# Shuffled pieces in one DMA issue, z beside x2 in alternate rows, a first half image in two steps, and a count read early

## The chip, the cores and the metric

The kernel runs on one core of one Trainium2 chip. The metric is device time in microseconds (us) of one execution; 0.2% of it is 5.9 us. The engines are named as in the profile: PE (matmul), PEld (weight load of the same engine), DVE (vector), ACT (scalar), POOL (GpSimd) and SP (which here issues most DMAs).

## The reference, cut

An activation x of shape (4, 256, 64, 64), float32, passes four layers, each with a residual:

```python
x = x + attention(gn(x))            # layer 0: axial attention, batch norms
x = x + ternary_conv3x3(gn(x))      # layer 1: weights -1, 0, 1
x = x + binary_block(gn(x))         # layer 2, below
x = x + conv3x3(gn(x), W)           # layer 3: weights built from 64x64

def binary_block(x):
    x = channel_shuffle(x, 2)
    xa, xb = split(x, 2, axis=1)
    x2 = batchnorm(leaky_relu(gconv3x3(sign(x), w1, groups=2)))
    x3 = batchnorm(concatenate((x2 + xa, xb), axis=1))
    x3 = channel_shuffle(x3, 2)
    x4 = batchnorm(leaky_relu(gconv3x3(sign(x3), w2, groups=2)))
    x5a, x5b = split(x3, 2, axis=1)
    return concatenate((x4 + x5a, x5b), axis=1)
```

`gn` is a group norm with 32 groups. A channel shuffle interleaves the two halves of the channels: new channel 2i is old i, new channel 2i + 1 is old 128 + i. The batch norms take their statistics over all four images, so each is a point where the whole of the data has to be there.

## The kernel before

Channels lie on partitions (128 of them, P), so the 256 channels make two halves, t = 0 and 1; a channel half of one image is 128 x 4096 float32 (HW = 4096), held in two tiles of 128 x 2048. The four images are b = 0 to 3.

The attention of layer 0 leaves its two parts in DRAM, `at_d[0]` and `at_d[1]`. Layers 1 and 3 are one function, `conv_layer`, named "d" and "g", a Winograd convolution along the rows. For every image `prepare(b, t)` loads a channel half through `load_1` or `load_3`, sums its statistics (L1028 for the sum; L1086 and L1088 in the trace are the aggregate and the shift of its mean), `norm` turns these into a scale over groups with small matmuls into `pst` (L112, L122, L123), `transform` writes a padded half image (ACT, L1110) and its row transforms `dtr` or `gtr` (DVE, L963 to L976), and `chunk` runs the matmuls (L989, `dc` or `gc`), adds the results to the residual on DVE and calls `finish`. `rest()` runs the chunks of an image with the preparation of the next between them. For the first image all of `prepare`, `norm` and `transform` has to be done before the first matmul of the layer, in two steps: g begins with the channel half t = 1, d with t = 0, and the first 36 or more matmuls need that half only.

`load_1` (d) brings x in shuffled order with `load_shuffled` (L138 to L143), which issues two DMAs of 64 rows into alternate partitions; then, for `two` in 0 and 1, eight pieces of 128 x 512 of the attention's output, also through `load_shuffled`, each followed by one DVE operation (L1181). The pieces have tags a0 and a1 by their number, with two buffers each. `finish_1` stores the layer's result to `x2_d` (L1204) by POOL.

Layer 2 (names e_...) has two binary convolutions. A half image of signs lies in `e_pad`; `binary_rows` (L1241) makes its row transforms `e_tr` on DVE, four operations of 128 x 1056 for each of the two groups; `binary_conv` runs 72 matmuls a chunk (L1251) and six DVE operations (L1260 to L1266), one ACT copy and one ACT square. `images` runs four chunks an image with `prepare_1` or `prepare_2` of the next image between them. `rows_of` loads 33 rows of x2 into one of four slots (three of pool xp3, the fourth, every fourth load, of xp1). In `prepare_2` (L1450 to L1469) the half t = 1 gives signs only (L1468); t = 0 is scaled by ACT (L1455), gets the first convolution's result added by DVE (L1459), is stored to `z_d` (L1462, 128 rows), and gives signs. Both halves' signs go to both groups, and only then come the row transforms. All this needs the batch norm's affine after the last chunk of the first convolution (end of it L1408).

`load_3` (g) brings a half of x2 (L1494), then four times a piece of z and x2 in alternate partitions:

```python
a = ap_.tile([P, HW // 8], F32, name=f"x3_{b}_{t}_{half}_{q}", tag="a0")
nc.sync.dma_start(out=a[0:P:2, :], in_=z_d[b][64 * t : 64 * t + 64, part])
nc.sync.dma_start(out=a[1:P:2, :], in_=x2_d[b][P + 64 * t : P + 64 * t + 64, part])
nc.vector.scalar_tensor_tensor(
    xt[:, cols], a, sg[:, t, 0, b : b + 1], xt[:, cols], ALU.mult, ALU.add
)
```

(L1500 to L1505), all with tag a0, that is two buffers; for t = 0 a piece of y follows with tag a1 (L1507 to L1516).

The order on each engine is set by a scheduler that places instructions by priority and readiness as it models them; `tc.high_priority()`, `tc.keep_in_program_order(i)` and `tc.issue_after(i)` constrain it. A DMA waits on its issuing queue for its buffer, and whatever is behind it on that queue waits with it.

At the end a count of attention rows whose softmax sum left the safe range is formed (one matmul, one cast), read into registers on the engines, and compared: only if it is above zero is everything from the scores on done again in a general form. It is zero here, so that second copy isn't run.

Of the kernel before, what the change touches and what calls it, by code (L numbers as in the profile page):

```python
# [18 lines left out]
B = 4  # L19
# [21 lines left out]
def network(ctx: ExitStack, tc, x, wqkv, relm, relt, relw, relv, counts, masks, vecs, rowv, ab, w1, l2w1, l2w2, l3w, mats, out):  # L41
# [16 lines left out]

    at_d = [[scratch(f"at_d{two}{b}", [C, HW]) for b in range(B)] for two in range(2)]
    x2_d = [scratch(f"x2_d{b}", [C, HW]) for b in range(B)]  # L60
    z_d = [scratch(f"z_d{b}", [P, HW]) for b in range(B)]
    y_d = [scratch(f"y_d{b}", [P, HW]) for b in range(B)]

    u1_d = scratch("u1_d", [P, 2, 3, 6, C])
# [71 lines left out]
        nc.vector.tensor_tensor(c, beta, c, ALU.subtract)  # L136
        return s, c

    def load_shuffled(dst, src, t, step=P):

        for par in range(2):
            r = par * step + 64 * t
            nc.sync.dma_start(out=dst[par:P:2, :], in_=src[r : r + 64, :])  # L143

    def kernel_rows(u, w, a, c):

# [520 lines left out]
    def from_scores(general, keep):  # L667
# [487 lines left out]
        with ExitStack() as ph:  # L1155
            shift = {}

            def load_1(b, t, xh, ap_, st, mv, sp, pst, spare):
                for half in range(2):
                    load_shuffled(xh[half], x[b][:, bass.ts(half, HW // 2)], t)  # L1160
                for two in range(2):
                    if b == 0:
                        if t == 1:
                            prs[t, two] = value_norm(t, two, pst, "pst")
                    for half in range(2):
                        for q in range(4):
                            k = 4 * half + q
                            a = ap_.tile([P, HW // 8], F32, name=f"a_{b}_{t}_{half}_{q}_{two}", tag=f"a{q % 2}")
                            if two == 0:
                                load_shuffled(a, at_d[0][b][bass.ts(t, P), bass.ts(k, HW // 8)], 0, 64)  # L1170
                                xv = xh[half][:, bass.ts(q, HW // 8)]
                                av = a
                            else:

                                load_shuffled(
                                    a, at_d[1][b][bass.ts(t, P), q * 1024 + half * 512 : q * 1024 + half * 512 + 512], 0, 64
                                )
                                xv = xh[half].rearrange("p (n i) -> p n i", i=64)[:, :, bass.ts(q, 16)]
                                av = a.rearrange("p (n i) -> p n i", i=16)
                            kw = {"accum_out": st[:, k, 0:1]} if b == 0 and two == 1 else {}  # L1180
                            nc.vector.scalar_tensor_tensor(  # L1181
                                xv, av, prs[t, two][:, 0:1], xv, ALU.mult, ALU.add, **kw
                            )
                            if kw:
                                cols = slice(16 * q, 16 * q + 16)
                                nc.scalar.activation(
                                    spare[:, 1:33, 1 + 16 * q : 17 + 16 * q], xh[half].rearrange("p (n i) -> p n i", i=64)[:, :, cols],
                                    AF.Square, accum_out=st[:, k, 1:2],
                                )
                        if two == 1 and b > 0:  # L1190
                            half_stats(st, half, xh[half])
                if b == 0:
                    whole_stats(sp, mv, st)
                    shift[t] = small(keep, [P, 1])
                    nc.vector.tensor_tensor(shift[t], prs[t, 0][:, 1:2], prs[t, 1][:, 1:2], ALU.add)
                return shift[t], b == 0

            st_x2 = {}

            def finish_1(b, h, co, xh, sp, pst):  # L1200
                if h == 0:
                    st_x2[b, co] = sp.tile([P, NB, 6], F32, name=f"stx2_{b}_{co}", tag=f"sx{co}")
                half_stats(st_x2[b, co], h, xh)
                nc.gpsimd.dma_start(out=x2_d[b][bass.ts(co, P), bass.ts(h, HW // 2)], in_=xh)  # L1204
                if h == 1:
                    nc.vector.bn_aggr(mv2[:, b, co, :], st_x2[b, co].rearrange("p k s -> p (k s)"))
                    if co == 1:
                        gm, rs = norm_stats(sp, pst, mv2[:, b], slice(0, 2), M_GRPS, "2")
                        nc.vector.tensor_copy(gm2[:, b, :], gm)
                        nc.vector.tensor_copy(rs2[:, b, :], rs)  # L1210

            set_up, load_weights, prepare, norm, transform, rest, sp, pst = conv_layer(
                "d", ph, u1_d, "x0 a p0 x1 t0 u0 x2 x3 s u1 o x4 t2 t3 t1 x5 t4 t5 p1", M_GRPS, load_1,
                vec[:, V_L1B : V_L1B + 2], (0, 1), finish_1,
            )
            set_up()
            prepare(0, 0)
            load_weights(0, nc.sync)
            with tc.high_priority():
                norm(0, slice(0, 1))  # L1220
            transform(0, 0, 0)
            prepare(0, 1)
            load_weights(1, nc.sync)
            norm(0, slice(1, 2))
            transform(0, 1, 0)
            for t in range(2):
                transform(0, t, 1, True)
            rest()

        def binary_rows(v, pad):

            d = [pad[:, r : r + 31 : 2, :] for r in range(4)]
            for k, (i, j, op) in enumerate(
                ((0, 2, ALU.subtract), (1, 2, ALU.add), (2, 1, ALU.subtract), (1, 3, ALU.subtract))
            ):  # L1240
                nc.vector.tensor_tensor(v[:, k], d[i], d[j], op)  # L1241

        def binary_conv(psp, lp, parts, vs, q, dst, sums, squares, name):

# [26 lines left out]
        with ExitStack() as ph:  # L1271
# [51 lines left out]
            def inside(t, h, rows=slice(0, P)):  # L1323
                return pads[t][h][rows, 1 - h : 34 - h, 1:65]

            def transformed(b, t, h, i):
                s = 2 * ((2 * (B * i + b) + 1 - i + h) % 3) + t
                v = tslots[s].tile([P, 4, 16, 66], BF16, name=f"e_tr{i}_{b}_{t}_{h}", tag="tr")
                binary_rows(v, pads[t][h])
                return v  # L1330

# [116 lines left out]
            nc.vector.tensor_tensor(sa, sy1, half_scales(0, cy1), ALU.mult)  # L1448


            def prepare_2(b, h):
                for t in (1, 0):
                    xt = rows_of(b, t, h, "x3")
                    if t == 0:
                        nc.scalar.activation(  # L1455
                            xt, xt, AF.Identity, bias=cx[:, 0, b : b + 1], scale=sx[:, 0, b : b + 1]
                        )
                        xf = xt.rearrange("p h w -> p (h w)")
                        nc.vector.scalar_tensor_tensor(  # L1459
                            xf, y[b][:, 64 * 31 * h : 64 * (31 * h + 33)], sa, xf, ALU.mult, ALU.add  # L1460
                        )
                        nc.gpsimd.dma_start(out=z_d[b][:, bass.ts(h, HW // 2)], in_=xf[:, 64 * h : 64 * h + HW // 2])  # L1462
                    for g in range(2):
                        src = xt[64 * g : 64 * g + 64]
                        kw = {} if t == 0 else {
                            "bias": cx[64 * g : 64 * g + 64, 1, b : b + 1], "scale": sx[64 * g : 64 * g + 64, 1, b : b + 1]
                        }
                        nc.scalar.activation(inside(g, h, slice(64 * t, 64 * t + 64)), src, AF.Sign, **kw)  # L1468
                return [transformed(b, g, h, 1) for g in range(2)]  # L1469

            def chunk_2(b, q, vs):
                binary_conv(
# [14 lines left out]
        with ExitStack() as ph:  # L1487
            shift_y = small(keep, [P, B])

            def load_3(b, t, xh, ap_, st, mv, sp, pst, spare):  # L1490
                first = b == t == 0
                for half in range(2):
# [4 lines left out]
                    for q in range(4):  # L1497
                        part = bass.ts(4 * half + q, HW // 8)
                        cols = bass.ts(q, HW // 8)
                        a = ap_.tile([P, HW // 8], F32, name=f"x3_{b}_{t}_{half}_{q}", tag="a0")  # L1500
                        nc.sync.dma_start(out=a[0:P:2, :], in_=z_d[b][64 * t : 64 * t + 64, part])
                        nc.sync.dma_start(out=a[1:P:2, :], in_=x2_d[b][P + 64 * t : P + 64 * t + 64, part])
                        nc.vector.scalar_tensor_tensor(
                            xt[:, cols], a, sg[:, t, 0, b : b + 1], xt[:, cols], ALU.mult, ALU.add
                        )  # L1505
# [38 lines left out]
            for t in (1, 0):  # L1544
                transform(0, t, 1, True)
            rest()
        return bad

    bad = from_scores(False, keep)

    with ExitStack() as ph:
        sp = pool(ph, "z_s")
        far = small(sp, [P, 1])
        nc.vector.tensor_scalar(far, bad, -float(P), float(P), ALU.mult, ALU.add)
        count = sp.tile([1, 1], mybir.dt.int32, name="count")
        with ExitStack() as sums:
            psp = pool(sums, "z_ps", 1, PSUM)
            ps = psp.tile([P, 1], F32, name="pbad", tag="pbad")
            nc.tensor.matmul(ps[0:1], lhsT=far, rhs=mt[:, M_ALL, 0:1], start=True, stop=True)
            nc.vector.tensor_copy(count, ps[0:1])  # L1560
        lost = nc.values_load(count[0:1, 0:1], min_val=0, max_val=P)
        with tc.If(lost > 0):
            with ExitStack() as again:
                from_scores(True, pool(again, "z_keep"))


def _matrices():
# [107 lines left out]
```

## Time and profile before

| | us |
|---|---|
| median of 3 runs | 2942.96 (2942.49 to 2944.54) |
| profiled execution | 2940.49 |
| its span in the trace | 2938.6 |
| PE busy in the span | 2603.1 |
| DVE busy | 2050.6 |
| ACT busy | 1055.2 |
| granted PE clock, mean | 0.949 of full speed |

The span runs from the first to the last recorded instruction. "Busy" is the time with an instruction on the engine; for SP it isn't given, since issuing DMAs isn't counted as work. Stretches are quoted by their times in the span: attention ends near 1540, d runs to 2078, the first binary convolution to 2230, the second to 2392, g to the end.

### The profile page before, as it was taken

To read this page: it belongs to the slowest core of one execution; us is meant where nothing else is said; L and a number is where in the kernel's file an instruction comes from. 1 tells how busy PE (TensorE), PEld (TensorE's weight loads), DVE (VectorE), ACT (ScalarE), POOL (GpSimd) and SP (SyncE) were. 2 spreads that over 40 slices of the span, in tenths; PEclk is the share of its full clock that TensorE was granted. 3 is DMA by queue.
4 is the path that set the end of the run, shared out by engine and by line. 5 is a ranking of instruction groups with operands and counts; after the bars stand their busy time and mean duration, and the time that the engine had idled before them with its cause. 6 is when DMAs were issued, how large, how long until landed. Compare 5 with 4: busy or idle time off the path is not lost.

```text
span 2938.6 us, 77718 instructions
## 1 busy us (share of the span) xinstructions
PE 2603.1 (89%) x34248; PEld 1599.4 (54%) x34248; DVE 2050.6 (70%) x3661; ACT 1055.2 (36%) x2029; POOL 79.1 (3%) x153
## 2 busy tenths in 40 slices
PE   7999889899999688878766999999996968999997
PEld 4566556677777476666663444444453533444443
DVE  6555997566676356666667898895687968858742
ACT  4554445455555644454423011021247621110100
POOL 0000000000000100000000000000000000000000
PEclk9998999999999799989987999999997988999999
DMA  6767465555454877777774533432336763333100
GB/s 237 261 213 218 136 191 144 139 138 133 125 118 111 237 248 248 250 235 246 261 241 161 185 120 125 154 118 87 103 106 216 256 222 118 108 111 136 65 40 34
DMA packets 250266, 484.45 MB, mean 165 GB/s; under 512 B 29056, under 2 KB 129024, under 8 KB 225088
## 3 DMA queue, kind: packets, MB, share of 16 engines
q1 hardware_dynamic: 182304, 293.90, 31.3%
q10 hardware_dynamic: 58336, 125.85, 15.3%
q0 software_dynamic: 9280, 59.64, 5.1%
q8 instruction: 271, 4.44, 0.6%
q14 instruction: 75, 0.61, 0.1%
HBM read 282.96 MB, written 196.35 MB: 163 GB/s over the span
## 4 chain that ended last, share of the span: by engine, by line
PE 27%; issue 22%; DVE 7%; DMA 6%; ACT 3%; POOL 0%; SPq 0%; ACTq 0%; POOLq 0%; DVEq 0%
PE dc L989 15%; PE pc L1251 4%; DMA at_d<-o_False 3%; PE e_False L790 2%; PE den_False L841 2%; DVE pt L800 2%; PE pe_False L893 2%; DMA qc_False<-q_d 1%; PE pr_False L859 1%; PE pa_False L868 1%; ACT pt L830 1%; DVE o_False L877 1%; DMA x<-x_d 1%; ACT e_pad L1468 1%; ACT rb L861 1%
## 5 line engine op out<-in xcount | busy, mean ns | idle before, releaser
L989 PE MATMUL dc<-dtr,d_u 128*128 128x512 f32 x1152 | 504.6, 599 | 15.0 <-issue 9.6
L989 PE MATMUL gc<-gtr,g_u 128*128 128x512 f32 x1152 | 502.5, 598 | 11.7 <-DVE gtr L967 7.1
L479 DVE STREAM_TRANSPOSE t<-pd 128x1024 f32<-128x1024 f32 x256 | 303.9, 1226 | 107.7 <-PE pd L472 107.7
L989 PEld LDWEIGHTS gc<-gtr,g_u 128*128 128x128 f32 x1152 | 219.1, 191 | 287.7 <-issue 271.5
L989 PEld LDWEIGHTS dc<-dtr,d_u 128*128 128x128 f32 x1152 | 218.2, 191 | 285.8 <-issue 274.4
L472 PE MATMUL pd<-rm,qb 64*32 64x256 f32 x8192 | 283.5, 386 | 45.7 <-DVE t L479 42.6
L491 PEld LDWEIGHTS pq<-t,t 64*64 64x64 f32 x8192 | 258.8, 135 | 71.6 <-issue 48.5
L491 PE MATMUL pq<-t,t 64*64 64x64 f32 x8192 | 278.4, 220 | 17.5 <-issue 15.6
L1251 PE MATMUL pc<-e_tr,e_k 128*64 128x512 bf16 x2304 | 262.7, 388 | 19.3 <-DVE e_tr L1241 16.2
L495 ACT ACTIVATE o<-pq 128x512 f32<-128x512 f32 x256 | 152.2, 595 | 314.2 <-PE pq L491 314.1
L472 PEld LDWEIGHTS pd<-rm,qb 64*32 64x32 f32 x8192 | 156.6, 108 | 128.2 <-DVE t L479 60.8
L830 ACT ACTIVATE pt<-pt,sm 128x512 f32<-128x512 f32 x256 | 162.2, 709 | 174.1 <-DVE pt L800 174.1
L1251 PEld LDWEIGHTS <-e_k 128*64 128x64 bf16 x2304 | 144.8, 111 | 134.0 <-issue 24.7
L800 DVE TENSOR_TENSOR pt<-e_False,si_False 128x1024 f32<-128x1024 f32 x128 | 151.3, 1215 | 36.3 <-PE e_False L790 33.6
L790 PE MATMUL e_False<-qc_False,rw 32*128 32x256 f32 x1024 | 130.0, 469 | 31.5 <-DVE pt L800 19.2
L500 ACT ACTIVATE pq<-pq 128x512 f32<-128x512 f32 x256 | 149.8, 585 | 3.9
L1007 ACT COPY gc_c<-gc 128x512 f32<-128x512 f32 x32 | 18.6, 581 | 336.6 <-PE gc L989 336.4
L1007 ACT COPY dc_c<-dc 128x512 f32<-128x512 f32 x32 | 18.6, 583 | 327.0 <-PE dc L989 327.0
L280 PE MATMUL po<-xg,wt 128*128 128x512 f32 x256 | 123.2, 621 | 6.7 <-DVE st L287 5.1
L893 PE MATMUL pe_False<-pt,ve 128*32 128x64 f32 x4096 | 89.8, 239 | 41.9 <-issue 38.0
L295 PE MATMUL pv<-wt,xg 128*128 128x256 f32 x512 | 119.9, 382 | 0.0
L295 PEld LDWEIGHTS pv<-wt,xg 128*128 128x128 f32 x512 | 96.5, 191 | 33.4 <-issue 19.2
(399 smaller groups left out, 3385.2 us busy)
## 6 DMA issues: line engine op xcount, KB each, us to landing
si_False<-qk_d SPq DMA_DIRECT2D x64, 1024.0 KB
qk_d<-o ACTq DMA_DIRECT2D x124, 512.0 KB
x<-x_d SPq DMA_DIRECT2D x32, 1056.0 KB
a<-at_d SPq DMA_DIRECT2D x256, 128.0 KB
xa<-in_x SPq DMA_DIRECT2D x16, 1024.0 KB
vt_d<-vs ACTq DMA_DIRECT2D x32, 512.0 KB
q_d<-qs SPq DMA_DIRECT2D x64, 256.0 KB
qb<-q_d SPq DMA_DIRECT2D x128, 128.0 KB
```

Of the source, the lines that this page charges most:

```text
L295: nc.tensor.matmul(pv[:, j, :], lhsT=xg[:, t, pix], rhs=wt[:, t, C : 2 * C], start=(t == 0), stop=(t == 1),)
L472: nc.tensor.matmul(pds[t][32 * c : 32 * c + 32, m].rearrange("p j k -> p (j k)"), lhsT=q[rows, 2 * (gp % 2) + g, a, 32 * nb : 32 * nb + 32 ...
L479: nc.vector.transpose(ts[t][:, :, 32 * jh : 32 * jh + 32].rearrange("p a j b -> p j a b"), pds[t].rearrange("p m j k -> p j m k"),)
L491: nc.tensor.matmul(ps[rows, m, :], lhsT=ts[1][rows, n // 2, :, n % 2], rhs=ts[0][rows, n // 2, :, n % 2], start=True, stop=True, tile_posi ...
L495: nc.scalar.activation(o[:, :, 8 * k : 8 * k + 8, :], ps.rearrange("p n (a b) -> p a n b", b=2), AF.Copy, accum_out=acc[:, 0, gp, col : co ...
L500: nc.scalar.activation(psf, psf, AF.Square, accum_out=acc[:, 1, gp, col : col + 1])
L790: nc.tensor.matmul(es[x_ // 2][:, x_ % 2, :, :, par], lhsT=rw[rows, 63 - i : 127 - i].rearrange("p j r -> p (j r)"), rhs=q[rows, :, par, k ...
L800: nc.vector.tensor_tensor(dst, e, src, ALU.add)
L830: nc.scalar.activation(s, s, AF.Exp, scale=s2q[:, gp : gp + 1])
L893: nc.tensor.matmul(ps[32 * a : 32 * a + 32, m // 2, :, m % 2], lhsT=ve[:, 63 - i, :], rhs=pt[:, i // 2, a, :, i % 2], start=True, stop=Tru ...
L989: nc.tensor.matmul(ms[k], lhsT=u[t][:, dx, k, bass.ts(co, P)], rhs=vs[t][:, k, :, dx : dx + 64], start=(first and dx == 0), stop=(last and ...
L1251: nc.tensor.matmul(m[64 * g : 64 * g + 64], lhsT=parts[:, g, i, k, dx, :], rhs=vs[g][:, k, 8 * (q % 2) : 8 * (q % 2) + 8, dx : dx + 64], s ...
```

## The change

Four edits:

- `load_shuffled` is one DMA of 128 rows, whose source is a view that takes rows i and 64 + i (or 128 + i) in turn.
- `z_d` has 256 rows. z goes to its even rows, and `finish_1` stores the upper half of x2 a second time, to the odd rows (by POOL). So `load_3` takes a piece in one DMA of 128 rows. The tags of its t = 1 pieces alternate between a0 and a1, four buffers in all; t = 0 pieces stay in a0, beside y in a1.
- `prepare_2` loads t = 0 first, makes the signs of t = 1 first, and does the rest for the first half image of the first image in two steps of 16 or 17 rows: scale, add, signs and eight of the 16 row pairs each. `issue_after` holds the same work of each later half image behind the one before it. z is stored once a half image, after the steps.
- The count's matmul, cast and reading stand directly after d instead of at the end.

```diff
-    z_d = [scratch(f"z_d{b}", [P, HW]) for b in range(B)]
+    z_d = [scratch(f"z_d{b}", [C, HW]) for b in range(B)]
...
-    def load_shuffled(dst, src, t, step=P):
-        for par in range(2):
-            r = par * step + 64 * t
-            nc.sync.dma_start(out=dst[par:P:2, :], in_=src[r : r + 64, :])
+    def load_shuffled(dst, src, t):
+        rows = src.rearrange("(two i) f -> i two f", two=2)[64 * t : 64 * t + 64]
+        nc.sync.dma_start(out=dst, in_=rows)
...
                 nc.gpsimd.dma_start(out=x2_d[b][bass.ts(co, P), bass.ts(h, HW // 2)], in_=xh)
+                if co == 1:
+                    nc.gpsimd.dma_start(
+                        out=z_d[b].rearrange("(p two) f -> two p f", two=2)[1][:, bass.ts(h, HW // 2)], in_=xh
+                    )
...
             rest()
+            lost = None
+            if not general:
+                far = small(keep, [P, 1])
+                nc.vector.tensor_scalar(far, bad, -float(P), float(P), ALU.mult, ALU.add)
+                ps = pst.tile([P, 1], F32, name="pbad", tag="pst")
+                nc.tensor.matmul(ps[0:1], lhsT=far, rhs=mt[:, M_ALL, 0:1], start=True, stop=True)
+                count = keep.tile([1, 1], mybir.dt.int32, name="count")
+                nc.vector.tensor_copy(count, ps[0:1])
+                lost = nc.values_load(count[0:1, 0:1], min_val=0, max_val=P)
...
-        def binary_rows(v, pad):
-            d = [pad[:, r : r + 31 : 2, :] for r in range(4)]
+        def binary_rows(v, pad, first=0, n=16):
+            d = [pad[:, r + 2 * first : r + 2 * first + 2 * n - 1 : 2, :] for r in range(4)]
...
             def prepare_2(b, h):
-                for t in (1, 0):
-                    xt = rows_of(b, t, h, "x3")
-                    if t == 0:
+                xts = [rows_of(b, t, h, "x3") for t in range(2)]
...
+                signs(1, slice(0, 33))
+                vs = [slot(b, g, h, 1) for g in range(2)]
+                steps = ((0, 17, 0), (17, 33, 8)) if b == h == 0 else ((0, 33, 0),)
+                n = 16 // len(steps)
+                with ExitStack() as order:
+                    for i in ahead:
+                        order.enter_context(tc.issue_after(i))
+                    for r0, r1, pair in steps:
+                        xt = xts[0][:, r0:r1]
                         nc.scalar.activation(
                             xt, xt, AF.Identity, bias=cx[:, 0, b : b + 1], scale=sx[:, 0, b : b + 1]
                         )
                         xf = xt.rearrange("p h w -> p (h w)")
                         nc.vector.scalar_tensor_tensor(
-                            xf, y[b][:, 64 * 31 * h : 64 * (31 * h + 33)], sa, xf, ALU.mult, ALU.add
+                            xf, y[b][:, 64 * (31 * h + r0) : 64 * (31 * h + r1)], sa, xf, ALU.mult, ALU.add
                         )
+                        sign = signs(0, slice(r0, r1))
+                        for g in range(2):
+                            row = binary_rows(vs[g], pads[g][h], pair, n)
+                ahead[:] = [sign.ins, row.ins]
+                nc.gpsimd.dma_start(
+                    out=z_d[b].rearrange("(p two) f -> two p f", two=2)[0][:, bass.ts(h, HW // 2)],
+                    in_=xts[0].rearrange("p h w -> p (h w)")[:, 64 * h : 64 * h + HW // 2],
+                )
+                return vs
...
-                        a = ap_.tile([P, HW // 8], F32, name=f"x3_{b}_{t}_{half}_{q}", tag="a0")
-                        nc.sync.dma_start(out=a[0:P:2, :], in_=z_d[b][64 * t : 64 * t + 64, part])
-                        nc.sync.dma_start(out=a[1:P:2, :], in_=x2_d[b][P + 64 * t : P + 64 * t + 64, part])
+                        a = ap_.tile([P, HW // 8], F32, name=f"x3_{b}_{t}_{half}_{q}", tag=f"a{t * q % 2}")
+                        nc.sync.dma_start(out=a, in_=z_d[b][bass.ts(t, P), part])
```

`signs(t, rows)` makes both groups' signs of those rows, with the scale and shift of t = 1 in the same operation; `slot` is the tile allocation that `transformed` did.

## The prediction, made before the changed kernel was run

> **What bounds the kernel now.** I read the page first (which engine is full), then busy time by stretch (where it is not), then the waits of those stretches, then the DVE's timeline inside them.
>
> ```profile
> PE 2603.1 (89%) x34248; PEld 1599.4 (54%) x34248; DVE 2050.6 (70%) x3661; ACT 1055.2 (36%) x2029; POOL 79.1 (3%) x153
> a<-at_d SPq DMA_DIRECT2D x256, 128.0 KB
> x<-z_d SPq DMA_DIRECT2D x64, 128.0 KB
> x<-x_d SPq DMA_DIRECT2D x64, 128.0 KB
> ```
>
> The PE is 89% busy, so a saving counts only where the PE stands still. By stretch (PE first, DVE third, the PE's clock near the end):
>
> ```profile
> 1540.00:1600.00 60.00, 31.29 (x67) 15.17 (x68) 42.28 (x121) 20.90 (x43) 0.00 (x0) 0.69 0.62 202
> 1600.00:1700.00 100.00, 99.76 (x237) 44.06 (x236) 89.14 (x160) 12.17 (x15) 1.70 (x3) 1.00 0.47 147
> 2205.00:2250.00 45.00, 18.24 (x129) 10.94 (x127) 33.02 (x81) 27.38 (x24) 1.59 (x3) 0.67 0.50 174
> 2250.00:2360.00 110.00, 109.33 (x990) 63.87 (x986) 97.61 (x173) 79.51 (x66) 5.85 (x11) 1.00 0.76 268
> 2360.00:2440.00 80.00, 44.73 (x196) 20.96 (x197) 57.56 (x144) 19.76 (x36) 0.00 (x0) 0.74 0.60 207
> 2440.00:2920.00 480.00, 479.43 (x1129) 211.93 (x1128) 317.75 (x552) 50.72 (x61) 7.98 (x15) 1.00 0.25 85
> ```
>
> Both Winograd layers run full once begun. The PE misses 29, 27 and 35 us at three joints: start of the ternary layer (d), turn from the first to the second binary convolution, start of the last layer (g). The change touches all three. Waits of the last joint (2340 to 2440; total, times, longest):
>
> ```profile
> PE pst L112 <- DVE sm L1088: 22.8, 2, 12.7
> DVE gx L1503 <- DMA x<-x_d: 13.6, 6, 4.4
> PE gc L989 <- DVE gtr L967: 7.1, 1, 7.1
> DVE gx L1503 <- DMA gx<-x_d: 5.6, 2, 3.3
> DVE gx L1513 <- DMA yq<-y_d: 4.4, 3, 4.0
> SPq L1501 <- DVE gx L1503: 24.0, 10, 7.6
> ```
>
> The last row is the cause of the second: SP issues nothing until the DVE gives a piece buffer back. The DVE's timeline, with its idle times:
>
> ```profile
> 2357.40 0.75 DVE L1503 SCALAR_TENSOR_TENSOR gx<-x,sg,gx 128x512 f32<-128x512 f32 x1 [4.39 <-DMA x<-x_d]
> ...
> 2365.88 0.75 DVE L1503 SCALAR_TENSOR_TENSOR gx<-x,sg,gx 128x512 f32<-128x512 f32 x1 [2.74 <-DMA x<-x_d]
> 2368.65 0.75 DVE L1503 SCALAR_TENSOR_TENSOR gx<-x,sg,gx 128x512 f32<-128x512 f32 x1 [2.02 <-DMA x<-x_d]
> ...
> 2376.26 0.15 DVE L1088 TENSOR_TENSOR sm<-sm,sg 128x1 f32<-128x1 f32 x1
> ```
>
> Two pieces, a round trip, two pieces; then L1088, and 0.20 us later the PE.
>
> **What the Trainium skill says.** "DMA: Bandwidth & Descriptors", Anatomy of one DMA, gives about 2.0 us plus bytes over 436e9 per second for a transfer: as an estimate 2.3 us for 128 KB, 2.6 for 256 KB, so one issue of 128 rows should land about when two of 64 do. The trace agrees in a quiet moment (two 256 KB yq loads whose issues ended near 2413.0 and 2413.5 were used at 2415.11 and 2416.13, 2.1 and 2.6 us) but not in traffic: the pair of 64-row loads issued up to 2361.25 was used at 2368.65, 7.4 us. The same page, "Issuing engines are not separate DMA queues", says SP, ACT and POOL transfers share 16 engines; so the 8 MB more written by POOL load the SP's reads. "Perfetto Trace Analysis", DMA Instruction — HWDGE, says the profiled window of an issue leaves out the movement; hence landings here are read at the waiting instruction.
>
> **The change part by part.** I worked from the order of instructions that the changed program has on each engine.
>
> *Stage A, start of d.* L143 issues a piece twice, 0.54 us each; now once: 128 x 0.54 = 69 us of SP less over the layer, 16 dx issues too. SP isn't the bound except at the start. Before, the first sum (L1088, 1552.39) came after the last t=0 pieces at 1548.7 and 1550.1, which waited for loads, nine pieces standing after the attention's last statistics (1540.4). In the new order five pieces go ahead of the first L877, into DVE idle time (3.26 us before 1506.64 alone), and only two stand after the last statistics. What remains behind 1540.4: two pieces 1.5, L713 and small ones 1.9, square and sum about 1: L1088 near 1544.7, 7.7 earlier, and dc from 1559 instead of 1565.80.
> That stretch of 42 matmuls (21.1 us) then needs the other channel half. Its L1088 stood at 1584.74, behind seven pieces 1574.0 to 1582.4 paced by loads (idle 1.90, 0.55, 0.65, 0.39, 0.52, 1.73 between them). Without that pacing they end near 1570.5. But in the new order 12 pieces of image 1 and 3 or 4 statistics (12 x 0.68 + 3 x 0.65, about 10 us of DVE) stand between the sum and the row transform L963, where none stood. L963 thus comes near 1583 instead of 1591.39, the PE resumes near 1586 instead of 1593.51: **-7** (0 if image 1's pieces wait for loads; -10 if they don't queue up).
>
> *z in alternate rows.* prepare_2 stores z to even rows; finish_1 adds eight 1 MB POOL stores for the odd rows: 8 x 0.53 = 4.2 us of a POOL that is 97% idle. A dx buffer is freed one store later, 4.2 us from issue to landing (the x_d<-dx row); the PE has full work beside it there (DMA share 0.47 or less). Taken 0; were that cover gone, 4.2 per image, at most 13.
>
> *Stage B, end of the first binary convolution.* A late load landed at 2218.15, its two signs took 4.31 on ACT, and the copy for the last chunk ran behind them at 2223.68. In the new order that slot's load comes earlier and only one sign (2.15) stands there: 1.5 to 3, taken **-2**.
>
> *Stage C, second binary convolution.* The affine is done at 2234.4 (L1408). Before: 3 Identities (2.07 each), 3 L1459 (2.36 each) in a row, signs, rows; PE at 2244.45, then a 1.0 us wait. Half images halve each link: 1.12 + 1.27 + 2 signs 1.03 + rows 0.33, PE after about 5.4 instead of 10. But from 2236.6 to 2343.95 the DVE is about 95% busy with 7.4 us of preparing and 3.7 us a chunk, so the PE would soon wait for it: of 4.6 only about **-1** stays (0 to -5). Eight more small operations at 0.06 overhead add 0.5 to the DVE, inside this.
>
> *Stage D, start of g.* Tags a0/a1 alternate, so four buffers instead of two for t=1, and one issue a piece (0.45 + 0.60 before). All four pieces of the first half are there when the DVE arrives at 2343.95; the next four are in flight during those and a chunk (3.74), with one round trip of up to 7 us instead of three. Of the idle 4.39 + 2.74 + 2.02 = 9.2 most goes: L1088 near 2366.5, -9.5. The PE's wait of 10.04 for it goes with that; the next, gc at 2396.52, moves to 2387. Then the t=0 half: its yq round trips (last pair issued until 2418.10, used at 2422.60, behind a 1 MB gx load issued at 2414.84). In the new order that gx load precedes the pairs, and z needs half the issues: second L1088 2414 instead of 2426.12, gc resumes 2424.5 instead of 2436.60: -12 in all since the affine; of these the DVE's earlier end from C is 1. **-10** here without it (-5 to -14).
>
> *Count.* PE gets one 128x1 matmul at the d-to-e joint (L112 0.59 for two), 0.3 with its wait for the PSUM; SP waits for the cast about 2 us before the e_k of the second convolution, needed 150 us later; the TensorLoads on other engines stay at the end, so only matmul and cast leave there: **+0.2**.
>
> Sum: -7 - 2 - 1 - 10 + 0.2, about -20; I take -18, since C and D share the DVE. Span 2938.6 to about 2920.6, profiled run 2940.49 (1.9 around the span) to 2922.5; the median 2942.96 lies 2.5 over that run, so **2925**.
>
> **Rivals.**
> 1. *One joint pays only.* For: stage A's ten us of image-1 pieces are read from an order, and their loads may not have landed (before, 8 waits of 6.8 us for a<-at_d); stage D's yq buffers stay two. Against: SP has 69 us less to issue. A gives 0 and D -5 to -7 with B, C -2: -8, **2935**.
> 2. *The joints give all.* Image 1's pieces don't delay (-10), C's 4.6 stays: -27, **2916**.
> 3. *Slower: the one-issue shuffled load lands late.* Its rows come from two halves of the source, and if that costs, 20 pieces (8 of image 0, 12 of image 1) stand ahead of L963 at d's start with four buffers. At landing time T a piece comes every T/4 + 0.4. From about 1545, 20 pieces reach 1591 at 2.3 each, that is T = 7.6: from there A loses. With T = 12: 3.4 each, 68 us, PE resumes at 1615, +21, and D keeps -10 + 2 x 5 = 0: **2962**. Against: the longest landing read before is 7.4, in the heaviest stretch (share 0.76), and at d's start 0.62.
> 4. *The change doesn't do what it says:* the early count leaves the end as it was (the last TensorLoads follow the last store anyway); that is in the forecast.
>
> **How the numbers follow.** Forecast -18: 0.60. Joints give all: 0.08. One joint only: 0.19. Slower: 0.13. A measurement here tells 0.2% (5.9 us) from nothing: faster below 2937.1, slower above 2948.9. Rival 1 falls two thirds under the bound. Faster 0.60 + 0.08 + 0.12 = 0.80, same 0.08, slower 0.12. Range 2911 to 2940: rival 2 and rival 1 with their spread inside, rival 3 left out.
>
> **What would show it.** A: d's first pst L112 near 1545, dc's second stretch from about 1586, a<-at_d x128. B: no 4.3 us pair of signs at the end of pc1. C: first pc2 within 6 us of L1408. D: four L1544 (the old L1503) in a row, L1088 near 2366 less A, B and C, its wait on the PE under 3. Wrong if the PE's wait before pst at g is still near 10, if DVE idles for a<-at_d over 10 us at d's start, or if dc or gc have gaps inside their full stretches.

## The result, and the profile after

The changed kernel took 2939.97 us (median of 20 runs, 2926.74 to 2962.07), the one before 2942.72 in as many runs beside it: ratio 0.9989, 95% interval 0.9972 to 1.0007. That is no change that the measurement can tell from none, where 18 us less were forecast. The profiled execution took 2933.51, its span is 2931.7, 6.9 less than the span before; the interval says that this difference is not one to build on.

The page of the changed kernel: engines (busy time, share, instructions), and two lines of its DMA issues.

```profile
PE 2600.8 (89%) x34248; PEld 1595.5 (54%) x34248; DVE 2046.4 (70%) x3670; ACT 1056.1 (36%) x2032; POOL 83.2 (3%) x161
a<-at_d SPq DMA_DIRECT2D x128, 256.0 KB
```

The issues are halved as written, and the PE is as full as it was. Busy time by stretch, in the columns of the prediction (PE first, DVE third):

```profile
1540.00:1600.00 60.00, 37.74 (x86) 17.35 (x87) 51.75 (x132) 15.76 (x30) 0.00 (x0) 0.79 0.67 224
1600.00:1700.00 100.00, 97.59 (x228) 43.25 (x227) 83.68 (x152) 14.01 (x16) 2.22 (x4) 0.98 0.33 116
2205.00:2250.00 45.00, 29.71 (x240) 18.12 (x238) 34.23 (x91) 29.59 (x24) 1.06 (x2) 0.81 0.52 186
2250.00:2360.00 110.00, 100.11 (x902) 56.35 (x896) 99.61 (x179) 75.90 (x66) 6.38 (x12) 1.00 0.75 272
2360.00:2440.00 80.00, 45.08 (x155) 20.57 (x156) 56.24 (x138) 17.86 (x34) 0.00 (x0) 0.70 0.54 188
2440.00:2920.00 480.00, 474.61 (x1120) 209.98 (x1118) 311.98 (x543) 50.12 (x60) 8.51 (x16) 1.00 0.23 85
```

The gain and the loss can both be read here. At d's start the PE works 6 us more in the 60, at the turn of the two binary convolutions 11 more in the 45. But the two stretches that were full are full no longer: 97.6 of 100 in d, and 100.1 of 110 in the second binary convolution, where it was 109.3. (The last row is lower for another reason: the changed kernel's last matmul ends at 2914.6, inside the stretch.)

The waits of the last joint (2340 to 2440; total, times, longest):

```profile
PE pst L113 <- DVE sm L1088: 25.1, 2, 17.9
DVE gx L1544 <- DMA x<-z_d: 6.2, 4, 2.4
PE gc L989 <- DVE gtr L967: 6.7, 1, 6.7
DVE gx L1544 <- DMA gx<-x_d: 6.0, 1, 6.0
DVE gx L1554 <- DMA yq<-y_d: 6.0, 4, 3.1
```

The wait of the DVE for its pieces has halved (13.6 to 6.2). The PE's wait for L1088 hasn't shrunk in sum (22.8 to 25.1): the first of the two went from 10.0 to 7.1, the second from 12.7 to 17.9.

Single executions of one kernel spread over some 30 us. The traces say where much of this lies: the last den matmuls of the attention stand between 1489.1 and 1507.1 in the sixteen traces of this study, although the DVE's order up to there is the same in all. (SP's isn't quite: where `load_shuffled` issues once, three issues of x stand before that point instead of six.) What follows it repeats better where the program is the same (d's start 93.1 to 94.3 in the eight traces of kernels that leave it alone). So the traces are compared stage by stage from the last den matmuls (1499.3 before, 1493.6 after), each stage between two events on the PE or the DVE. `den` are the attention's softmax sums, `pc` the sums of a binary convolution, `psg` the small matmuls with scale and shift between the two; d's full stretch begins when the second channel half is there.

| us | before | changed |
|---|---|---|
| A: last den to d's full stretch | 94.2 | 92.7 |
| d, to the first pc matmul | 493.2 | 498.5 |
| first binary convolution, to its last psg matmul | 141.8 | 134.2 |
| turn, to the first pc of the second | 15.9 | 10.4 |
| second convolution, to g's first piece on DVE | 99.5 | 113.4 |
| from there to the end | 594.7 | 589.0 |
| sum | 1439.3 | 1438.1 |

The sum is 1.2 less, which fits the 0.9989. Some 20 us are gained and some 19 lost, and each loss stands right behind a gain.

### The profile page after: what moved, and what is told of

The parts are those of the page before. It is cut to its first block, busy times and chain, and to the rows that moved or that the text cites. A ratio compares the mean times of both kernels' runs of the same rounds, so it can differ in the third digit from the quotient of the medians.

```text
span 2931.7 us, 77330 instructions
## 1 busy us (share of the span) xinstructions
PE 2600.8 (89%) x34248; PEld 1595.5 (54%) x34248; DVE 2046.4 (70%) x3670; ACT 1056.1 (36%) x2032; POOL 83.2 (3%) x161
## 4 chain that ended last, share of the span: by engine, by line
issue 22%; PE 21%; DMA 9%; DVE 9%; ACT 4%; POOL 0%; SPq 0%; ACTq 0%; POOLq 0%; DVEq 0%
PE dc L989 12%; DMA at_d<-o_False 3%; PE e_False L790 2%; DMA x<-x_d 2%; PE pe_False L893 2%; DMA a<-at_d 2%; PE den_False L841 1%; PE pr_False L859 1%; DVE pt L800 1%; ACT e_pad L1480 1%; PE pa_False L868 1%; DMA qc_False<-q_d 1%; DVE dx L1181 1%; DVE o_False L877 1%; DVE e_tr L1254 1%
## 5 line engine op out<-in xcount | busy, mean ns | idle before, releaser
L790 PE MATMUL e_False<-qc_False,rw 32*128 32x256 f32 x1024 | 131.5, 477 | 29.8 <-DVE pt L800 16.1
L868 PE MATMUL pa_False<-pt,vb 128*32 128x64 f32 x4096 | 98.7, 239 | 22.5 <-DVE o_False L877 14.9
```

The costliest lines, as they stand in the source:

```text
L790: nc.tensor.matmul(es[x_ // 2][:, x_ % 2, :, :, par], lhsT=rw[rows, 63 - i : 127 - i].rearrange("p j r -> p (j r)"), rhs=q[rows, :, par, k ...
L868: nc.tensor.matmul(ps[32 * a : 32 * a + 32, m, :], lhsT=vb[n // 16][:, n % 2, a, :, n // 2 % 8], rhs=pt[:, :, a, n, :], start=True, stop=T ...
```

## The experiments

Thirteen kernels ran in fourteen experiments (E10 is E4 again), in four groups, each beside fresh runs of the kernel before. Stages in us; the ratio is of the times, with its 95% interval (it isn't the ratio of the two medians, from which it differs by up to 0.24%); "sum" is from the last den to the end. The pins in the names are the `issue_after` lines of `prepare_2`.

| kernel | A | d | conv 1 | turn | conv 2 | g | sum | ratio |
|---|---|---|---|---|---|---|---|---|
| before | 94.2 | 493.2 | 141.8 | 15.9 | 99.5 | 594.7 | 1439.3 | 1 |
| changed | 92.7 | 498.5 | 134.2 | 10.4 | 113.4 | 589.0 | 1438.1 | 0.9989 (0.9972 to 1.0007) |
| E1 steps only | 93.8 | 493.2 | 133.7 | 10.4 | 113.6 | 589.8 | 1434.4 | 1.0013 (0.9995 to 1.0030) |
| E2 no steps | 90.4 | 498.1 | 140.6 | 15.9 | 99.1 | 589.7 | 1433.8 | 0.9973 (0.9959 to 0.9987) |
| E3 z only | 94.1 | 492.5 | 141.1 | 15.9 | 99.2 | 589.9 | 1432.8 | 0.9991 (0.9971 to 1.0012) |
| E4 pieces only | 90.3 | 497.8 | 139.3 | 15.9 | 99.5 | 597.3 | 1440.2 | 1.0049 (1.0027 to 1.0072) |
| E5 load order | 93.2 | 493.0 | 133.8 | 15.9 | 110.6 | 594.3 | 1440.8 | 1.0016 (1.0001 to 1.0031) |
| E6 steps, no pins | 93.9 | 493.2 | 133.9 | 13.3 | 105.1 | 594.4 | 1433.7 | 0.9995 (0.9980 to 1.0010) |
| E7 steps, old load order | 93.6 | 493.2 | 138.0 | 10.4 | 107.9 | 594.3 | 1437.4 | 1.0017 (1.0002 to 1.0031) |
| E8 z and load order | 94.3 | 492.6 | 134.5 | 15.9 | 107.9 | 591.0 | 1436.1 | 1.0011 (0.9996 to 1.0026) |
| E9 pieces, first image | 84.5 | 492.5 | 140.0 | 15.9 | 99.2 | 592.3 | 1424.4 | 0.9980 (0.9965 to 0.9995) |
| E10 pieces only, again | 91.7 | 497.8 | 138.8 | 15.9 | 99.2 | 595.6 | 1439.1 | 1.0040 (1.0025 to 1.0054) |
| E11 z, two buffers | 94.2 | 492.5 | 138.6 | 16.0 | 99.2 | 595.2 | 1435.7 | 1.0001 (0.9985 to 1.0016) |
| E12 joined | 82.7 | 493.0 | 134.5 | 13.3 | 104.9 | 591.9 | 1420.4 | 0.9933 (0.9912 to 0.9955) |
| E13 changed, no pins | 90.4 | 495.2 | 134.6 | 13.3 | 105.6 | 592.2 | 1431.3 | 0.9980 (0.9962 to 0.9998) |
| E14 changed, first image | 86.4 | 493.2 | 134.9 | 10.4 | 114.1 | 586.5 | 1425.4 | 0.9913 (0.9892 to 0.9935) |

A stage has one trace behind it, a ratio 6 to 22 runs beside 18 to 59 of the kernel before. How far a stage repeats can be read from the kernels that leave its code alone: d 492.5 to 493.2 and the second convolution 99.1 to 99.5, but the first convolution 138.6 to 141.8 and g 589.8 to 597.3. The kernels with z's edit and four buffers have g at 586.5 to 592.2, so the few us that it gains there overlap with this spread.

**E1, prepare_2 alone.** The diff's prepare_2, binary_rows and slot, put into the kernel before.

```diff
-                for t in (1, 0):
-                    xt = rows_of(b, t, h, "x3")
...
+                xts = [rows_of(b, t, h, "x3") for t in range(2)]
...
+                signs(1, slice(0, 33))
...
+                steps = ((0, 17, 0), (17, 33, 8)) if b == h == 0 else ((0, 33, 0),)
...
```

> The kernel before with the new prepare_2 alone (load order, signs of t=1 first, two steps for the first half image, issue_after). Theory 1 (the new prepare_2 wins about 5.6 us at the turn and gives back more inside the second binary convolution, by the order on ACT): the PE starts the second convolution about 10 us after the last psg matmuls instead of 15.9, but the stretch from that start to g's first L1503 is 110 to 114 us instead of 99.5; the time is the same or up to 8 us longer than before. Theory 2 (the stretch in the trace of after was long by chance of its transfers, or because of z's stores): the stretch stays near 100 to 104 and the time falls by 4 to 6 us.

Theory 1 held: turn 10.4, second convolution 113.6, no gain in the ratio. The first convolution came as a surprise: it is 8 us shorter here too, so this belongs to prepare_2 as well. The three stages together are 257.2 before, 257.7 here and 258.0 in the changed kernel: what the new prepare_2 gains in two stages it pays in the third. E1's g is 4.9 shorter as well, although `load_3` is untouched; why isn't shown, and E6 and E7 don't repeat it.

**E2, the changed kernel with the old prepare_2.**

```diff
-                xts = [rows_of(b, t, h, "x3") for t in range(2)]
...
+                for t in (1, 0):
+                    xt = rows_of(b, t, h, "x3")
...
```

> The changed kernel with the old prepare_2 (its store into z's even rows). Theory 1: the turn takes 15 to 16 us again, the second convolution about 100, and g's first matmuls come earlier than in the changed kernel; time 5 to 12 us below before. Theory 2: the time is that of the changed kernel or up to 5 us longer.

The three stages are the old ones but for the spread of the first, and the time is 0.27% below before. E1 and E2 agree: theory 2 (chance, or z's stores) falls.

**E3, z alone.** The edits of `z_d`, of `finish_1` and of z's store too; shown is `load_3`.

```diff
...
-                        nc.sync.dma_start(out=a[0:P:2, :], in_=z_d[b][64 * t : 64 * t + 64, part])
-                        nc.sync.dma_start(out=a[1:P:2, :], in_=x2_d[b][P + 64 * t : P + 64 * t + 64, part])
+                        nc.sync.dma_start(out=a, in_=z_d[b][bass.ts(t, P), part])
...
```

> The kernel before with z in 256 rows, the second stores of x2, one issue a piece in load_3 and tags a0/a1 for t=1. Theory 1 (the start of g pays as forecast, and the loss is elsewhere): PE's wait for g's first L1088 falls from 10.0 us to under 4, g's full stretch begins 6 to 10 us earlier counted from the last psg matmuls, and the time falls by 5 to 10 us. Theory 2 (the second half of g's start, its x2 and y loads, sets the end anyway): the first L1088 comes earlier but the full stretch moves by less than 4 us.

Between the theories: the PE's first wait fell from 10.0 to 2.8, and L1088 came 22.3 us after the first piece instead of 32.5 (counted to the PE's start behind it; 21.6 to 24.1 in all seven traces with four buffers, 31.6 to 32.9 in the eight with the old `load_3`). Of these 10 us 4.4 are left at the full stretch and 4.8 at the end, and the ratio doesn't show them. The DVE's timeline (line 1509 is load_3's piece here) shows where the rest went:

```profile
2370.85 0.75 DVE L1509 SCALAR_TENSOR_TENSOR gx<-x,sg,gx 128x512 f32<-128x512 f32 x1 [2.84 <-DMA x<-z_d]
...
2377.56 0.75 DVE L1509 SCALAR_TENSOR_TENSOR gx<-x,sg,gx 128x512 f32<-128x512 f32 x1 [4.80 <-DMA x<-z_d]
```

These are t = 0 pieces, which still have two buffers; they stand on the DVE ahead of the last chunk and of gtr, and the round trip that t = 1 no longer waits for is waited for here. The PE's timeline has a second part of it:

```profile
2420.19 0.59 PE L112 MATMUL pst<-sm,mt 128*128 128x1 f32 x2 [12.48 <-DVE sm L1088]
2420.64 2.05 PE L989 MATMUL gc<-gtr,g_u 128*128 128x512 f32 x2
2422.48 0.42 PE L122 MATMUL pst<-sm,mt 128*128 128x1 f32 x2
2422.77 2.76 PE L989 MATMUL gc<-gtr,g_u 128*128 128x512 f32 x4
2425.37 0.28 PE L123 MATMUL pst<-sm,mt 128*128 128x1 f32 x2
```

Before, L123 followed L122 after 0.28 us; now four gc matmuls stand between, 2.6 us. They are work that has to be done, but the chain to gtr runs through L123: from the second L112 to the full stretch it is 13.1 us, where it was 10.3.

**E4 and E10, one issue a piece alone, twice.**

```diff
-        for par in range(2):
-            r = par * step + 64 * t
-            nc.sync.dma_start(out=dst[par:P:2, :], in_=src[r : r + 64, :])
+        rows = src.rearrange("(two i) f -> i two f", two=2)[64 * t : 64 * t + 64]
+        nc.sync.dma_start(out=dst, in_=rows)
...
```

> The kernel before with load_shuffled in one issue alone. Forecast's stage A: from the last den matmuls of attention to the second stretch of dc 7 us less than before (before 95.6, changed 94.1 in its trace), time 5 to 7 us below before. Rival: image 1's pieces ahead of L963 and PE's waits for L1088 at the turns of images inside d (4.0 us in the changed kernel's trace, 0.2 before) take it back: the time is within 3 us of before.

> The kernel with one issue a piece in load_shuffled alone, a second time. Its runs were 0.49% above before while its trace was only 0.9 us longer behind the attention. If this belongs to the kernel, the runs lie 0.3 to 0.6% above before again; if it came with that measurement, they lie within 0.2%. Stages in the trace: A 90.3, d 497.3 within 1 us.

(The first text counts A from a point 1.4 us earlier than the table.) Stage A gains 3.9 and 2.5, d loses 4.6 both times, and the kernel is slower by 0.49 and 0.40%. The rival held in the trace, and the time is worse than it says: the sums differ from before by +0.9 and -0.2 only. The other 7 to 14 us (6.5 and 9.0 by the medians, 13.5 and 12.0 by the ratios) aren't settled, since an execution without a profile has no stages. They are no fixed price of these issues either: E2 has the same ones beside z's edit, loses 4.9 in d, and is 0.27% faster than before, of the size of its sum (-5.5).

**E5, the load order alone.**

```diff
+                xts = [rows_of(b, t, h, "x3") for t in range(2)]
                 for t in (1, 0):
-                    xt = rows_of(b, t, h, "x3")
+                    xt = xts[t]
```

> The kernel before, with prepare_2's two loads in the order t=0, t=1 and nothing else of the change (so that the fourth slot of rows_of, with its own pool, holds a t=1 tile). Theory a (the load order gives the 7.6 us of the first binary convolution and costs nothing later): pc1 to the last psg 134 us instead of 141.8, second convolution to g's first piece near 100, time 5 to 8 us below before. Theory b (the load order is what makes ACT wait for its loads in the second convolution): that stretch is over 108 us and the time is not below before.

Theory b, and half of theory a: this line gives the whole gain of the first convolution (133.8) and takes it back with interest in the second (110.6). Waits of that stretch (2242 to 2353), and the ACT line that carries them:

```profile
ACT e_pad L1469 <- DMA x<-x_d: 8.0, 2, 6.0
PE pc L1251 <- ACT pc_o L1259: 7.2, 2, 6.3
```

```profile
2297.61 2.15 ACT L1469 ACTIVATE e_pad<-x,sm,sm 64x2112 bf16<-64x2112 f32 x1 [5.98 <-DMA x<-x_d]
```

A sign waits 6 us for its rows, the copy of the PE's sums stands behind it on ACT, and the PE waits 6.3 us for the copy. In the kernel before ACT waits for no load in this stretch, and the PE for no copy longer than 0.2 us.

**E6 and E7, the new prepare_2 without pins, and with the old load order.** Both are E1 with one edit.

```diff
-                    for i in ahead:
-                        order.enter_context(tc.issue_after(i))
```

> The new prepare_2 alone, without the issue_after pins. Theory a (the pins hold ACT and DVE work of later half images back): the second convolution falls from 113.6 us (with pins) to near 100, with the turn still at 10.4. Theory b (load order or the place of the signs): it stays over 108.

```diff
-                xts = [rows_of(b, t, h, "x3") for t in range(2)]
+                xts = [rows_of(b, t, h, "x3") for t in (1, 0)][::-1]
```

> The new prepare_2 alone, with its two loads in the old order t=1, t=0. Theory a (load order): the first convolution is 141 us again, and the second stays long, over 108, if the pins are the cause. Theory b (load order is the cause of the long second convolution): it falls to near 100.

Neither is the sole cause. Without pins the second convolution falls from 113.6 to 105.1 and the turn rises from 10.4 to 13.3; with the old load order it falls to 107.9 and the first convolution rises to 138.0, near where the old `prepare_2` has it. The three stages are 252.3 without pins and 256.3 with the old order: only leaving the pins out is a clear net gain in the trace (4.9 against before), though the ratio 0.9995 doesn't show it. Both left out together weren't run, and by what path the pins lengthen the stage isn't shown.

**E8, z and the load order.** Both edits as shown.

> The kernel before with z in 256 rows and one issue a piece of it (with tags a0/a1), and the load order t=0, t=1; load_shuffled, prepare_2's steps and the count as before. If the two gains stand beside each other: first convolution 134, g's first L1088 about 22 us after its first piece instead of 32, end of attention's last den matmuls to the end near 1426 us instead of 1439, time 8 to 14 us below before. Rival (the earlier end of the first convolution is waited out in the second, which DVE and ACT bound): 1432 as with z alone.

The rival, and a little worse: three stages of 258.3, and a sum of 1436.1 where z alone has 1432.8.

**E9, one issue a piece for the first image only.** `load_shuffled` gets a parameter `one`: where it is true it issues once, else twice. x of the first image is loaded so too.

```diff
-                                load_shuffled(a, at_d[0][b][bass.ts(t, P), bass.ts(k, HW // 8)], 0, 64)
+                                load_shuffled(a, at_d[0][b][bass.ts(t, P), bass.ts(k, HW // 8)], 0, 64, one=b == 0)
...
```

> The kernel before with one issue a piece for the first image only (the other three keep two). If the 4.6 us lost inside d come from DVE work of the next image that now stands ahead in DVE's order and waits there for its x load, they go: d from its full start to its end 492 to 493 us as before, and stage A keeps 3 us or more (last den to d's full start 91 or less, before 94.2); from den to the end 1435 to 1436 against 1439.3. If they come from the pieces' transfers themselves at the first image, d stays near 497.

Better than expected: d is 492.5, and stage A 84.5, 9.7 us less than before. (The sum is 14.9 less, but 1.8 of that lie in the first convolution and 2.4 in g, within the spread of those stages.) The PE's timeline of E9 at d's start (line 993 is the conv matmul here):

```profile
1560.40 17.12 PE L993 MATMUL dc<-dtr,d_u 128*128 128x512 f32 x34 [8.51 <-issue]
...
1584.91 15.27 PE L993 MATMUL dc<-dtr,d_u 128*128 128x512 f32 x31 [3.29 <-DVE dtr L971]
```

and the same of the changed kernel:

```profile
1555.61 14.76 PE L989 MATMUL dc<-dtr,d_u 128*128 128x512 f32 x30 [8.51 <-issue]
1571.67 0.38 PE L113 MATMUL pst<-sm,mt 128*128 128x1 f32 x2 [1.31 <-DVE sm L1088]
...
1586.26 14.07 PE L989 MATMUL dc<-dtr,d_u 128*128 128x512 f32 x28 [7.34 <-DVE dtr L967]
```

From first dc to the full stretch 24.5 us against 30.7. In E9 two pieces stand between the second L1088 (there L1092) and the row transform; in the changed kernel nine pieces of image 1, six of them waiting 0.2 to 0.9 us for loads, and three statistics (1571.83 to 1583.7).

**E11, z with two buffers.** E3 with `tag="a0"` for all pieces.

> z in 256 rows and one issue a piece, but all pieces with tag a0, two buffers. If g's first L1088 comes earlier because of the buffers, it stands about 32 us after the first piece again; if because of the halved issues, at 22 to 25.

Neither, but between them: L1088 stands 28.6 us after the first piece. Of the 10.2 that E3 gained, 3.9 come from the halved issues and 6.3 from the buffers. At the end nothing is left of it (595.2).

**E12, E13, E14: parts of the change joined.** E12 is the changed kernel without pins and with one issue a piece for image 0 only; E13 drops the pins alone, E14 the later images' single issues alone.

> The changed kernel without issue_after, and with one issue a piece for the first image only. From the stages: z -6.5, prepare_2 without pins -5.6, the first image's pieces -3 to -4, count 0: den to the end near 1424 us against 1439.3 before and 1438.1 changed; time 10 to 16 us below before. Rival: they are not additive (the second convolution's stretch is bound by DVE and ACT whatever begins earlier), 1430 or more.

> The changed kernel without issue_after, all else kept. Theory (the pins cost what the joined version gained in the second convolution): turn 13.3 us, second convolution to g's first piece 105 instead of 113.4, together 5 to 6 less; den to the end near 1432 against 1438.1, time 0.1 to 0.3% below before. Rival (the pins matter only beside the old pieces): 1437 or more, time as the changed kernel's.

> The changed kernel with one issue a piece for the first image only, pins kept. Theory (the other three images' pieces cost it the joint and 5 us inside d): d's full start 84 us or less after the last den (92.7 in the changed kernel), d 492, second convolution still 113; den to the end near 1425, time 0.3 to 0.6% below before. Rival (only the 5 us inside d go): 1433.

In their direction all three theories held. E12 and E14 gained more time than expected (23 and 24 us by the medians), E14's stage A is 86.4 where 84 or less was expected, and only six runs stand behind each of the two. One condition, `one=b == 0`, takes the changed kernel from 0.9989 to 0.9913. Leaving out the pins gives 0.9980, which isn't told apart from 0.9989, though its sum is 6.8 less; both together, 0.9933, aren't told apart from the first alone. E14 and E12 are faster than the kernel before by 0.9 and 0.7%, and than the changed one by 0.8 and 0.6%. The stages explain 12.7 us of the 22 between the changed kernel and E14. The rest lies ahead of the last den, where the two traces differ by 2.9, or in executions without a profile; its cause stays open.

## Why the prediction was wrong, point by point

Most of the gains came where they were forecast. What failed is what the sum put behind them. In stage C it took -1 as what stays, and the turn's -5.5 was followed by +13.9 in the second convolution; and for the later images inside d it had no term at all, where 5.3 us were lost. The halves of A and D behind their first waits were mis-sized as well.

**Stage A: the size, and a step left out.** The first half came in part: counted from den, L1088 and dc are 4.4 us earlier (forecast 7.7; in E9, with the same edit for this image, 6.5). The second half was put at 10 us of DVE between the sum and L963, on the assumption that image 1's pieces find their loads landed. It was 12.2 (1571.47 to 1583.68), since six of the nine pieces behind the sum waited for their loads; two more stood among the steps of the sum itself. From the first dc to the full stretch it thus took 30.7 us instead of 27.7. "-7" was -1.5 in this trace, -2.5 to -3.9 in the four others with the same issues; with the old issues for image 1, in E9, it is -9.7. The bound named (0 if the pieces wait) was the right one to take. That the PE resumed at 1586.26, as forecast ("near 1586"), is luck: the attention ended 5.7 us earlier in this execution.

**Images 1 to 3: priced at nothing, and wrong.** "SP isn't the bound except at the start" was true and beside the point. Halving the issues made the scheduler place the later images' pieces earlier on the DVE. Waits inside d (1600 to 2080) of the changed kernel:

```profile
DVE dx L1181 <- DMA dx<-in_x: 22.5, 4, 10.2
```

```profile
PE pst L113 <- DVE sm L1088: 4.0, 3, 2.4
```

and of the kernel before:

```profile
DVE dx L1181 <- DMA dx<-in_x: 3.4, 1, 3.4
```

```profile
PE pst L112 <- DVE sm L1088: 0.2, 1, 0.2
```

The DVE takes its instructions in order: the Trainium skill has it in "Perfetto Trace Analysis", Tensor Engine Instruction ("ACT/DVE/GPSIMD are strict FIFO"), and the trace agrees: a piece waits 9.66 us until 1776.05 and nothing runs on the DVE meanwhile. A piece that reads the next image's x stands there until that x is loaded; SP waits to issue that load until the stores of a tile have landed (46.4 us for x_d<-dx and 25.7 for z_d<-dx in d). Behind the piece stand the sums that the PE waits for. That the issues of images 1 to 3 are the cause is shown: E9 and E14, without them, have d at 492.5 and 493.2, E4 and E10, with nothing else, at 497.8 (E13, which has them too, at 495.2). How the 22.5 us become 4.0 on the PE is argued only: the longest of these PE waits, 2.41 us at 1667.98, follows a wait for x of just 1.50 us, so the place of the pieces counts beside the wait. In d that is +5.3 us by stage; in time E14's condition is worth 22 us to the changed kernel. The prediction read the new order for the first image's start; the other images decided.

**Stage B: right sign, wrong account.** -2 was forecast for one sign instead of two behind the late load. The pair is still there, and still waits for its load, in the kernel before and in the changed one:

```profile
2218.17 4.31 ACT L1468 ACTIVATE e_pad<-x,sm,sm 64x2112 bf16<-64x2112 f32 x2 [4.60 <-DMA x<-x_d]
```

```profile
2208.65 4.30 ACT L1480 ACTIVATE e_pad<-x,sm,sm 64x2112 bf16<-64x2112 f32 x2 [5.38 <-DMA x<-x_d]
```

Counted from the first pc matmul it starts at 123.9 us instead of 131.5: the load came earlier, and that is the whole of the -7.6. E5 shows it to be a loan: the same line of code that brings this load forward lets a sign wait 6 us for another load in the second convolution.

**Stage C: the step that failed most.** The turn gained 5.5 (forecast 4.6), and it was said that "of 4.6 only about -1 stays (0 to -5)". The end at 0 had no ground: that a full DVE eats a gain was seen (it was busy for 99.4 of the 107.4 us named, 93% and not 95), that the new order could make the second convolution itself slower was not asked. Waits of the changed kernel in it (2229 to 2343):

```profile
ACT e_pad L1480 <- DMA x<-x_d: 6.1, 2, 5.0
PE pc L1265 <- ACT pc_o L1273: 4.7, 5, 1.7
PE pc L1265 <- DVE pc_o L1275: 2.7, 3, 1.2
```

B and C together are +0.8 instead of -3. E5, E6 and E7 show two causes in that stage, the load order and the pins.

**Stage D: the first wait right, the second mis-sized.** L1088 came 10.6 us earlier after g's first piece (forecast 9.5). The t = 0 half was to follow by as much or more. It kept two buffers, its pieces now wait in the place of the others (E3), and the DVE waits 6.0 us at 2401.29 for an x2 load of 1 MB, ahead of the y pairs. Its L1088 came 8.3 us earlier after the first piece, and 3.6 of these went again behind it, where L124 stands behind gc matmuls (13.9 us from the second L113 to the full stretch, before 10.3). At the end it is -5.7 of -10, a size that the spread of g leaves uncertain.

The fit for a transfer that the prediction took from the Trainium skill ("DMA: Bandwidth & Descriptors", Anatomy of one DMA) is given there for POOL's path, while these loads are SP's. Of them the trace shows the 2.1 to 2.6 us and the 7.4 us that the prediction read, and no run here tests the fit itself.

**Count:** 0.5 instead of 0.2, with nothing gained at the end, as said.

The sum was thus -19.8 forecast (-18 taken) against -1.2: +5.5 in A, +5.1 in d beyond the count, +3.8 in B and C, +4.3 in g. The prediction's own sign of being wrong, gaps in dc's full stretch, is what the trace shows (4.0 us in three). Rival 1 described the outcome best, by one of its reasons, that image 1's loads may not have landed. Rival 3's mechanism, a late landing of the one-issue load, isn't what happened: E9 uses the same load for the first image and has the lowest sum of all the parts run alone. Its outcome, slower, is nevertheless what one issue a piece does when it is made for every image and nothing else is changed (E4, E10).

## What to carry to other kernels

When a scheduler places instructions by modelled costs, a cheaper transfer can move its consumers forward on an engine that runs in order; read the new order for every iteration, not the first, and look for operations whose other operand comes late. A gain before a stage that an engine fills may not last through it: sum the stages on both sides of the joint, as the three here, which stay at 252 to 260 us in all sixteen traces. And where edits come in one change, run each with and without: here the changed kernel without the later images' single issues is 0.9% faster than before, and with them not told apart from it.

## What the runs showed that was not expected

A short wait on the PE can cost more than its length. In d of the changed kernel a wait of 2.41 us is followed by slower matmuls:

```profile
1667.98 0.46 PE L113 MATMUL pst<-sm,mt 128*128 128x2 f32 x2 [2.41 <-DVE sm L1088]
1668.30 2.06 PE L989 MATMUL dc<-dtr,d_u 128*128 128x512 f32 x2
```

Two matmuls of 128x512 take 2.06 us, in the full stretch 1.10 (1794.03). The granted clock is 0.50 from 1668.15 to 1671.56 and 1.00 behind that. At d's start a wait of 1.31 us left the next pair at 1.11. The length of the wait alone doesn't decide it: in E2 a wait of 2.06 us (1661.53) left the next pair at 1.10, in E4 one of 0.30 us (1577.78), soon after another of 1.66, was followed by a pair of 2.06.
